# First head of a graph attention layer: two half tiles to a buffer, and a new order of the work around them

## Chip, core, metric

One core of a Trainium2 chip. The metric is the device time of one execution in microseconds (us), as the median of several runs. The profile is of one further execution, whose own time is given beside its span.

## What is computed

Four graph layers, one after the other, on a matrix `x` of 2708 nodes by 512 features with a 0/1 adjacency matrix of 2708 x 2708. Each layer adds to `x` what it computes from `h = relu(layernorm(x))`. The change is in layer 2, graph attention with 8 heads of 64 features:

```python
Wh = jnp.einsum('nd,hdo->hno', x, W)
f1 = jnp.einsum('hno,ho->hn', Wh, a1)
f2 = jnp.einsum('hno,ho->hn', Wh, a2)
e = jax.nn.leaky_relu(f1[:, :, None] + f2[:, None, :], negative_slope=ALPHA)
e = jnp.where(adj[None, :, :] > 0, e, NEG_INF)
attention = jax.nn.softmax(e, axis=-1)
h_prime = jnp.einsum('hnm,hmo->hno', attention, Wh)
out = jax.nn.elu(h_prime)
```

Here `x` stands for that layer's `h`. Layers 0, 1 and 3 multiply the adjacency matrix (layer 1 a part of it) with a matrix of 512 columns.

## The kernel before

**Attention without exponentials of matrices.** The exponential of a leaky ReLU of a sum is a maximum of two products of one factor for the node of the row and one for the node of the column. So the exponentials are taken of vectors only: `exps_nodes` makes `er` from f1, `exps2` makes `ef` and `ec` from f2. The row factors of a head are turned by TensorE and sent to a DRAM row `rT` (`row2`: a transpose into `f_ps`, a copy by ScalarE into a tile `row`, and a DMA that ScalarE issues), and one DMA (`load_row1`, tile `rb`, issued by SyncE) spreads a head's row over all 128 partitions. A weight tile for 128 neighbours is then one VectorE instruction (`make`): the maximum of the row and `ec`, times the 0/1 pattern `vT` of the adjacency matrix, into a tile `t2` of 128 x 2708 with four buffers (`TILES`).

**Units and steps.** A unit is a head with a range of columns. The first and the last head are split in two halves of columns at `cut` (1408 and 1300 columns), the six heads between them are whole, so there are ten units. Each has 22 steps, one for each chunk of 128 nodes (NC = 22; the last has 20 nodes). In step s the planner's loop first issues the load of the features for step s + 6 (in groups of three), the scaling of the features for step s + 3 (`scale`, ScalarE, tile `whs`, four buffers), the weights for step s + 3 (`make`), then TensorE's products of step s (`multiply`: 16 instructions for the features into `av`, 8 for the row sums into `sums`, 32 columns wide so that four run beside each other in the array), and then what `plan` holds for the step. In the middle heads, and in the first half of the last one, 17 of 22 steps take their row sums from a comparison that ScalarE makes (`compare`, tile `b`).

**Neighbour sums.** Beside the first head's 44 steps, TensorE also counts over neighbours (`count_neighbors`, `adj_sums`, 17 sets of 8 products). Each set needs four pieces of the pattern in bf16 (`mask`, ScalarE, tile `x` with five buffers; the fourth piece of later sets is made by VectorE). `fourths` are the borders of the pieces.

**Early and late chunks.** The first EARLY = 11 chunks get their exponentials and rows while layer 2's dense part still runs (`rows2`, six steps behind the loads of that part). In the dense part a chunk c is loaded at step c, normalized, turned, multiplied (`product2`, at c + 3, which also makes the products with a1 and a2: `wh_a`, one on VectorE and one on GpSimd) and summed (`sums2` at c + 4, VectorE, into `f` and `f12`). At chunk `LATE` = 17 the first features are loaded, and at chunks 18, 19 and 20 the first three scalings and weights are made. The exponentials and rows of the late chunks are planned for the first head's steps 4 to 9, `split` (bf16 parts of the factors, on ScalarE and VectorE) for step 9, and the load of the second half's row for step 10.

**Tails.** The 20 nodes of the last chunk are put together for the six middle heads into one tile of 120 rows: `load_tails` (30 small DMAs and more on SyncE's queue, planned for step 12), `exp_tails` on ScalarE (step 30) and `make_tails` on VectorE (step 36).

**What sets the order.** The program's order is a priority. A scheduler at compile time puts each engine's instructions into a fixed order by a model of when each is ready, so an instruction can be ahead of its place in the code: in the trace the tails' scaling runs at 855.0 us, some ten steps before its place. `tc.issue_after(ins)` puts what follows behind `ins` on that engine's queue. Each engine then works through its own fixed order and waits at an instruction whose inputs or buffer are not ready.

The change touches `rows2` with `LATE`, `make`, `load_row1`, `row2`, `mask`, `cut`, the list `stages2`, and the plan and the loop over `steps`.

Of the kernel before, what the change touches and what calls it, by code (L numbers as in the profile page):

```python
# [8 lines left out]
F32 = mybir.dt.float32  # L9
F32R = mybir.dt.float32r  # L10
BF16 = mybir.dt.bfloat16
# [9 lines left out]
P = 128  # L21

R = 128
# [3 lines left out]
TILES = 4  # L27
# [17 lines left out]
def fast_layers(  # L45
# [36 lines left out]
    nc = tc.nc  # L82
    N, D = x_in.shape
    H, _, O = w2.shape
    NC = -(-N // R)
# [6 lines left out]
    def rows(c):  # L92
        return min(R, N - c * R)
# [18 lines left out]
    EARLY = NC // 2  # L112
# [363 lines left out]
    with ExitStack() as ring_ctx:  # L476
# [20 lines left out]
        def save2(c):  # L497
            move(nc.scalar, x2[c * R : c * R + rows(c), :], sums1.pop(c)[: rows(c)])
# [9 lines left out]
        with tc.tile_pool(name="l0", bufs=2) as wk, ExitStack() as ctx_l0:  # L508
            units = [(g, m) for g in range(len(groups)) for m in range(NC)]
# [213 lines left out]
            for i in range(2):  # L723
                first_unit = (1 + 2 * i) * NC
                at(first_unit - 10, fusion.load, i)
                steps = [(fusion.turn, i, f) for f in range(NF) if i]
# [174 lines left out]
        def before1(c):  # L901
# [8 lines left out]
            x2,  # L910
            lambda *args: product2(*args),
            False,
            [(3, lambda c: save_last2(c)), (4, lambda c: sums2(c)), (6, lambda c: rows2(c))],
            scalar=True,
        )
        ahead = [(m, emit_step, step, NC, stages2) for step, m in enumerate(AHEAD)]
# [14 lines left out]
    ABOVE = 1.0 + 2.0**-21  # L931
    S = 32

    cut = EARLY * R // 8 * 8
    units = [(h, 0, N) for h in range(H)]
    units[-1:] = [(H - 1, 0, cut), (H - 1, cut, N)]
    units[:1] = [(0, 0, cut), (0, cut, N)]
# [3 lines left out]
    def in_tails(u, m):  # L941
        return m == NC - 1 and units[u][0] in middle

    steps = [
        (u, m)
        for u in range(len(units))
        for m in ((NC - 1, *range(NC - 1)) if 1 < u < len(units) - 1 else range(NC))
    ]

    def by_side(u, m):  # L950
        return 1 < u < len(units) - 1 and m in BY_SIDE
# [11 lines left out]
    at = at_ctx.enter_context(tc.tile_pool(name="att", bufs=1, reuse_waits="tile"))  # L963
# [10 lines left out]
    nc.gpsimd.memset(one6, 0.0)  # L974
    nc.gpsimd.memset(one6[:, 6:7], 1.0)
    row, weight, wh, whs, acc, sides, made, scaled = {}, {}, {}, {}, {}, {}, [], {}

    def load_row1(h, lo, hi):

        if lo == 0:  # L980
            row[h] = at.tile([R, N], F32, name="rb", bufs=2)
        src = rT[h : h + 1, lo:hi]
        nc.sync.dma_start(
            row[h][:, lo:hi],
            bass.AP(tensor=src.tensor, offset=src.offset, ap=[[0, R], [1, hi - lo]]),
        )

    LINES = len(middle) * last_rows
    assert LINES <= P
# [55 lines left out]
    def scale(s):  # L1045

        u, m = steps[s]
        h, q = units[u][0], rows(m)
        if in_tails(u, m):
            whs[s] = tails_w[:LINES, middle.index(h)]  # L1050
            return
        t = at.tile([R, O + S], F32, name="whs", bufs=4)
        by = ef[:q, m, h : h + 1]
        ins = nc.scalar.activation(t[:q, :O], wh.pop((u, m))[:q], AF.Copy, scale=by)  # L1054
        if not by_side(u, m):
            ins = nc.scalar.activation(t[:q, O:], one6[:q], AF.Copy, scale=by)
        scaled[s] = ins.ins
        whs[s] = t[:q]

    def make(s):  # L1060
        u, m = steps[s]
        h, lo, hi = units[u]
        q = rows(m)
        g, k = where[m]
        if in_tails(u, m):
            weight[s] = tails_row[:LINES]
            made.append(made[-1])
            return
        t = at.tile([R, N], F32, name="t2", bufs=TILES)
        ins = nc.vector.scalar_tensor_tensor(  # L1070
            t[:q, : hi - lo],
            row[h][:q, lo:hi],
            ec[:q, m, h : h + 1],
            vT[g][:q, k, lo:hi],
            op0=ALU.max,
            op1=ALU.mult,
        )
        weight[s] = t[:q]
        made.append(ins.ins)
# [47 lines left out]
    def sums2(c):  # L1127
        n = rows(c)
        f = small.tile([P, 2, H], F32, name="f")

        with tc.issue_after(firsts[min(c + 1, NC - 1)]):
            for i in range(2):
                t = products.pop((c, i))
                nc.vector.tensor_reduce(f[:n, i, :], t[:n, :, : O // (1 + i)], AX.X, ALU.add)  # L1134

        nc.vector.tensor_scalar(
            f12[:n, c, :],
            f[:n].rearrange("p i h -> p (i h)"),
            F_MAX + 1.0,
            -F_MAX - 1.0,  # L1140
            op0=ALU.min,
            op1=ALU.max,
        )

    def row2(c):
        pf = ps.tile([P, R], F32, name="f_ps", tag="ps")
        nc.tensor.transpose(pf[:H], er[:, c], ident[:R, :R])
        r = at.tile([H, R], F32, name="row", bufs=2)
        nc.scalar.copy(r, pf[:H])
        nc.scalar.dma_start(rT[:, c * R : (c + 1) * R], r)  # L1150

    def exps_nodes(cs):
        nc.scalar.activation(er[:, cs], f12[:R, cs, :H], AF.Exp, scale=1.0 - SLOPE2)

    def exps2(cs):
        nc.scalar.activation(ef[:, cs], f12[:R, cs, H:], AF.Exp)
        nc.scalar.activation(ec[:, cs], f12[:R, cs, H:], AF.Exp, scale=SLOPE2 - 1.0)
# [27 lines left out]
                    parts2[:, at_i[0] : at_i[-1] + 1 : len(kinds), i, heads], src  # L1185
                )

    LATE = NC - 5
    early_rows = [(0, EARLY // 2 + 1), (EARLY // 2 + 1, EARLY)]

    def rows2(c):
        for first, end in early_rows:
            if c == end - 1:
                exps_nodes(slice(first, end))
            for n in range(2):
                if first <= first + 2 * (c - end + 1) + n < end and c >= end - 1:
                    row2(first + 2 * (c - end + 1) + n)
        if c == EARLY - 1:
            exps2(slice(0, EARLY))
        if c == EARLY + 1:  # L1200
            load_row1(*units[0])
            split(0, EARLY)

        if c == LATE:
            load_wh(0)
            load_wh(GROUP)
        if LATE < c <= LATE + 3:
            scale(len(made))
            make(len(made))

    def save_last2(c):
        if c < len(spans[-1]):
            save2(spans[-1][c])
# [5 lines left out]
    tails = tails_ctx.enter_context(  # L1219
        tc.tile_pool(name="tails", bufs=1, side="right", reuse_waits="tile")  # L1220
    )
# [140 lines left out]
    fourths = [0, cut // 2, cut, (cut + N) // 2, N]  # L1362
    counted, masks = [], {}
# [4 lines left out]
    def mask(i, j):  # L1368
        m = BY_SIDE[i]
        q = rows(m)  # L1370
        g, k = where[m]
        own = slice(fourths[j], fourths[j + 1])
        n = own.stop - own.start
        if j == 3 and m >= EARLY:
            t = masks[i, j] = tails.tile([P, fourths[1]], BF16, name="mask", bufs=2)
            nc.vector.tensor_copy(t[:q, :n], vT[g][:q, k, own])
            return
        t = masks[i, j] = common.tile([P, D], F32, name="x", bufs=XBUFS).bitcast(BF16)
        nc.scalar.copy(t[:q, :n], vT[g][:q, k, own])
# [40 lines left out]
    def behind(s, fn, *args):  # L1420
        plan.setdefault(s, []).append((fn, args))

    behind(4, exps_nodes, slice(EARLY, NC))
    behind(4, exps2, slice(EARLY, NC))
    for c in range(EARLY, NC):
        behind(4 + (c - EARLY) // 2, row2, c)
    behind(10, load_row1, *units[1])
    behind(9, split, EARLY, NC)
    behind(12, load_tails)
    behind(30, exp_tails)  # L1430
    behind(36, make_tails)
    behind(30, load_l3_weights)
# [41 lines left out]
    for s in range(len(steps)):  # L1474
        if s == (len(units) - 3) * NC + 1:
            tails_ctx.close()
            first3 = ctx.enter_context(
                tc.tile_pool(name="first3", bufs=1, side="right", reuse_waits="tile")
            )
            rings3 = [first3]  # L1480
            b3 = first3.tile([P, D], F32, name="b3")
            nc.sync.dma_start(
                b3, bass.AP(tensor=bias3.tensor, offset=bias3.offset, ap=[[0, P], [1, D]])
            )
            e3_ctx = ctx.enter_context(ExitStack())
            e3 = e3_ctx.enter_context(
                tc.tile_pool(name="e3", bufs=2, side="right", reuse_waits="tile")
            )
        if s + 6 < len(steps) and (s + 6) % NC % GROUP == 0:
            load_wh(s + 6)  # L1490
        if s + 3 < len(steps):
            scale(s + 3)
            make(s + 3)
        if s + 1 < len(steps):
            compare(s + 1)
        multiply(s)
        multiply_sides(s - 1)
        for fn, args in plan.pop(s, ()):
            if fn in (load_l3_weights, spread_nodes, split):
                with tc.issue_after(made[s]):  # L1500
                    fn(*args)
            elif fn is mask:
                with tc.issue_after(scaled[s + 2]), tc.issue_after(made[s]):
                    fn(*args)
            else:
                fn(*args)
# [715 lines left out]
```

## Time and profile before

| what | us |
|---|---|
| median of 3 runs (1745.71 to 1747.05) | 1746.12 |
| the profiled execution | 1746.28 |
| its span from first to last instruction | 1744.5 |
| TensorE busy in the span | 1721.5 (99%) |
| VectorE busy | 1317.9 (76%) |
| ScalarE busy | 845.4 (48%) |
| GpSimd busy | 248.3 (14%) |

On the time axis of the span, layer 2's dense part ends at 810.6 us, the first half of the first head runs to 863, the second to 903, and the heads to 1356. The engines are called PE (TensorE's products), PEld (its weight loads), DVE (VectorE), ACT (ScalarE), POOL (GpSimd) and SP (SyncE, of which only the DMA queue matters here). A stretch in which PE is busy is not one in which it works at its peak, since its ends are modelled, and its clock can be lowered: the share of the full clock that it was granted is a column of its own. Waits are attributed to what came last.

Durations that come up again, in the trace before:

| instruction | us |
|---|---|
| weights of 128 x 1408 (DVE) | 1.60 from start to next start |
| weights of 128 x 1300 | 1.49 |
| weights of 128 x 2708 | 3.03 |
| piece of the pattern (ACT, `x`) | 0.76 |
| scaling of a step's features (ACT, two instructions) | 0.34 and 0.31 |
| row: copy (ACT) and issue of its DMA | 0.25 and 0.27 |
| loading ACT's table for the exponential | 1.28 |
| broadcast of the first half's row, from issue to first use | 4.3 |

### The profile page before, as it was taken

Reading aid. Unit: us, or ns where it says so; the run is one execution under the profiler, and the core shown is the slowest. Engines: PE = TensorE matmul, PEld = TensorE weight load, DVE = VectorE, ACT = ScalarE, POOL = GpSimd, SP = SyncE. Lnnn points to the kernel's source line nnn. Section 1 sums busy time; section 2 is a strip of 40 time slices with the busy share of each in tenths; the row PEclk is TensorE's granted clock in tenths of the full one; section 3 lists DMA queues with packets and bytes.
Section 4 is the critical chain, followed back from the end, with each engine's and each line's share of the span. In section 5 each row is a group of like instructions: output and inputs, shape, how many; then the busy total and the mean of one; then the engine's idle time right before and its main releaser. Section 6 shows DMA issues by size and latency. Waiting matters only on the chain.

```text
span 1744.5 us, 29430 instructions
## 1 busy us (share of the span) xinstructions
PE 1721.5 (99%) x11280; PEld 1074.9 (62%) x11280; DVE 1317.9 (76%) x1902; ACT 845.4 (48%) x1556; POOL 248.3 (14%) x252
## 2 busy tenths in 40 slices
PE   8999999999999999999999999999999999999998
PEld 5567777744458888644675665433434544588886
DVE  7759889865555556888899999999999787633334
ACT  5446767622210000266878888888794656400000
POOL 1003323311111111365000000000001222100000
PEclk9999999999999999999999999999999999999999
DMA  8446666444551111342420221022022444313221
GB/s 292 136 122 198 205 204 188 139 115 124 121 142 49 49 49 53 118 129 94 131 64 15 61 64 47 26 65 66 16 68 77 135 132 128 113 36 109 74 73 41
DMA packets 167227, 177.37 MB, mean 102 GB/s; under 512 B 84127, under 2 KB 106591, under 8 KB 166060
## 3 DMA queue, kind: packets, MB, share of 16 engines
q1 hardware_dynamic: 144428, 131.99, 27.4%
q10 hardware_dynamic: 18808, 33.37, 5.0%
q0 software_dynamic: 3840, 10.03, 1.5%
q8 instruction: 90, 1.47, 0.4%
q14 instruction: 61, 0.50, 0.1%
HBM read 111.64 MB, written 55.36 MB: 96 GB/s over the span
## 4 chain that ended last, share of the span: by engine, by line
PE 42%; DVE 9%; issue 3%; ACT 2%; DMA 2%; SPq 1%; POOL 0%; ACTq 0%; DVEq 0%; POOLq 0%
PE av L1315 15%; PE acc L425 12%; DVE t L1070 7%; PE self_ps L187 4%; PE nb_ps L187 4%; PE sums L1315 3%; DMA x<-x 1%; PE hT_ps L246 1%; PE wh_ps L187 1%; DVE wh_a L1117 1%; ACT b L1088 1%; PE av_ps L1253 1%; DVE f L1134 1%; DVE ln_st L219 0%; DMA rb<-rT 0%
## 5 line engine op out<-in xcount | busy, mean ns | idle before, releaser
L1070 DVE SCALAR_TENSOR_TENSOR t<-rb,ec,vT 128x2708 f32<-128x2708 f32 (+2 forms) x214 | 510.8, 2456 | 8.3 <-PE sums L1315 6.4
L1315 PE MATMUL av<-t,whs 128*32 128x451 f32 (+5 forms) x4432 | 444.6, 514 | 6.0 <-DVE t L1070 4.7
L425 PE MATMUL acc<-halves,kt 128*128 128x512 f32 x1848 | 423.6, 390 | 1.0 <-DVE kt L873 1.0
L425 PEld LDWEIGHTS acc<-halves,kt 128*128 128x128 f32 x1848 | 346.1, 188 | 75.3 <-DVE kt L873 2.6
L1088 ACT ACTIVATE b<-t,eb 128x2708 bf16<-128x2708 f32 (+1 forms) x119 | 285.1, 2396 | 33.2 <-DVE t L1070 33.1
L1315 PEld LDWEIGHTS av<-t,whs 128*32 128x32 f32 (+1 forms) x4432 | 192.4, 110 | 169.6 <-issue 119.4
L425 PE MATMUL acc<-halves,ar 128*128 128x512 f32 x924 | 243.8, 414 | 0.0
L425 PEld LDWEIGHTS acc<-halves,ar 128*128 128x128 f32 x924 | 172.5, 188 | 58.3 <-issue 20.8
L223 ACT ACTIVATE ln_rs<-ln_mv,eps 128x1 f32<-128x1 f32 x88 | 25.7, 295 | 305.9 <-DMA x<-x 199.0
L873 DVE SCALAR_TENSOR_TENSOR kt<-lastr,index,vT 128x512 fp32r<-128x512 int16 (+3 forms) x154 | 112.8, 747 | 72.4 <-PE acc L425 72.2
L1539 DVE CAST kt<-vT 128x512 fp32r<-128x512 uint8 (+3 forms) x154 | 56.4, 368 | 130.6 <-PE acc L425 130.6
L1267 POOL TENSOR_SCALAR z<-y 128x512 f32<-128x512 f32 x22 | 43.7, 1987 | 628.7 <-DVE y L1260 623.1
L558 DVE TENSOR_TENSOR_SCAN cum<-ai,deg 128x512 int16<-128x512 int32 (+2 forms) x110 | 128.3, 1170 | 0.0
L601 ACT ACTIVATE cum<-cum,limit 128x512 int16<-128x512 int16 (+3 forms) x132 | 88.0, 667 | 51.5 <-DVE deg L566 49.4
L1315 PE MATMUL sums<-t,whs 128*32 128x325 f32 (+4 forms) x952 | 103.9, 449 | 0.0
L1054 ACT ACTIVATE whs<-wh,ef 128x64 f32<-128x64 f32 x214 | 72.5, 341 | 53.0 <-PE sums L1315 18.9
L219 DVE BATCH_NORM_STATS2 ln_st<-x 128x6 f32<-128x512 f32 x88 | 60.5, 689 | 49.7 <-DMA x<-x 35.1
L187 PE MATMUL wh_ps<-w2s,hT 128*128 128x512 f32 x168 | 76.0, 595 | 0.9 <-ACT hT L248 0.9
L187 PE MATMUL h_ps<-w0s,hT 128*128 128x512 f32 x168 | 76.5, 598 | 0.0
L1315 PE MATMUL sums<-b,parts 128*32 128x338 bf16 (+2 forms) x884 | 76.2, 308 | 0.0
L552 ACT ACTIVATE ar<-ai 128x512 fp32r<-128x512 int32 (+2 forms) x132 | 75.0, 568 | 1.8 <-DMA ai<-in_adj 1.3
L187 PE MATMUL self_ps<-wfs,hT 128*128 128x512 f32 x168 | 75.7, 593 | 0.0
(211 smaller groups left out, 1956.2 us busy)
## 6 DMA issues: line engine op xcount, KB each, us to landing
x<-x SPq DMA_DIRECT2D x105, 256.0 KB
ai<-in_adj SPq DMA_DIRECT2D x84, 256.0 KB
x<-x ACTq DMA_DIRECT2D x84, 256.0 KB
x<-in_x SPq DMA_DIRECT2D x42, 256.0 KB
rb<-rT SPq DMA_DIRECT2D x7, 1354.0 KB
wh<-whd SPq DMA_DIRECT2D x63, 96.0 KB
packed<-two POOLq DMA_DIRECT2D x44, 128.0 KB, 3.0
whd<-wh SPq DMA_DIRECT2D x21, 256.0 KB
```

The costliest lines, as they stand in the source:

```text
L187: nc.tensor.matmul(po[:n], lhsT[:, f, :n], w[:, f, :], start=(f == 0), stop=(f == NF - 1))
L219: nc.vector.bn_stats(st[:n], xc[:n])
L425: nc.tensor.matmul(acc[:R], weight[:, k * R : (k + 1) * R], parts[:, i, :], start=(m == 0 and i == 0), stop=(m == NC - 1),)
L552: nc.scalar.activation(ar[:, :gw], ai[:, :gw], AF.Square, accum_out=squares[:R, m, g : g + 1])
L558: nc.vector.tensor_tensor_scan(cum[:n, :gw], ai[:n, :gw], ai[:n, :gw], 0.0 if g == 0 else deg[:n, m : m + 1], op0=ALU.add, op1=ALU.max,)
L601: nc.scalar.activation(cum[:n, :gw], cum[:n, :gw], AF.Sign, bias=limit[:n], scale=-1.0, accum_out=signs[:n, m, g : g + 1],)
L873: nc.vector.scalar_tensor_tensor(by_chunk(kt, cs), lastr[:, cs[0] * R : (cs[-1] + 1) * R].rearrange("p (c r) -> p c r", r=R), index[:R, m ...
L1054: ins = nc.scalar.activation(t[:q, :O], wh.pop((u, m))[:q], AF.Copy, scale=by)
L1070: ins = nc.vector.scalar_tensor_tensor(t[:q, : hi - lo], row[h][:q, lo:hi], ec[:q, m, h : h + 1], vT[g][:q, k, lo:hi], op0=ALU.max, op1=AL ...
L1088: nc.scalar.activation(b[:q, : hi - lo], weight[s][:, : hi - lo], AF.Sigmoid, bias=eb[:q, m, h : h + 1], scale=STEEP,)
L1315: nc.tensor.matmul(p[j * S : (j + 1) * S, : b - a], lhsT, rhs[:, part * size + a : part * size + b], start=(s % NC == 0), stop=(s % NC == ...
L1539: nc.vector.tensor_copy(by_chunk(kt, cs), pattern(m, cs))
```

## The change

The first head is cut at 1352 columns and no longer at 1408, so that two half tiles (1352 and 1356 columns) fit into one weight tile: odd steps of unit 0 use the second half of the buffer of the step before. In the dense part, scaling and weights start at chunk 13 and not at 18, with up to three scalings and eight weights (`LATE + 2 * TILES`). Within a step of the dense part `rows2` comes ahead of the sums, and the last chunk's sums are put behind the seventh weight. In the loop, weights may run up to five steps ahead until the early ones are made. The late chunks' exponentials are planned three steps later and put behind the scaling of step s + 2 = 9; their rows are planned three steps later and have three buffers; the second row's load moves from step 10 to 13, `split` from 9 to 12, and `load_tails` from 12 to 19 and behind the second row's load. `cut` is also that of the last head.

```diff
-            [(3, lambda c: save_last2(c)), (4, lambda c: sums2(c)), (6, lambda c: rows2(c))],
+            [(3, lambda c: save_last2(c)), (6, lambda c: rows2(c)), (4, lambda c: last_sums2(c))],
...
-    cut = EARLY * R // 8 * 8
+    cut = N // 2 // 8 * 8
+    assert cut <= EARLY * R and 2 * cut <= N
...
+    row_loads = []
...
-        nc.sync.dma_start(
+        ins = nc.sync.dma_start(
...
+        row_loads.append(ins.ins)
...
-        t = at.tile([R, N], F32, name="t2", bufs=TILES)
+        if u == 0 and m % 2:
+            t = weight[s - 1, cut]
+        else:
+            t = at.tile([R, N], F32, name="t2", bufs=TILES)
+            if u == 0:
+                weight[s, cut] = t[:, cut:]
...
+    def last_sums2(c):
+        with ExitStack() as behind:
+            if c == NC - 1:
+                behind.enter_context(tc.issue_after(made[6]))
+            sums2(c)
...
-        r = at.tile([H, R], F32, name="row", bufs=2)
+        r = at.tile([H, R], F32, name="row", bufs=3)
...
-    LATE = NC - 5
+    LATE = EARLY + 1
...
         if LATE < c <= LATE + 3:
-            scale(len(made))
+            scale(len(whs))
+        if LATE < c <= LATE + 2 * TILES:
             make(len(made))
...
-            t = masks[i, j] = tails.tile([P, fourths[1]], BF16, name="mask", bufs=2)
+            t = masks[i, j] = tails.tile([P, N - fourths[3]], BF16, name="mask", bufs=2)
...
-    behind(4, exps_nodes, slice(EARLY, NC))
-    behind(4, exps2, slice(EARLY, NC))
+    behind(7, exps_nodes, slice(EARLY, NC))
+    behind(7, exps2, slice(EARLY, NC))
     for c in range(EARLY, NC):
-        behind(4 + (c - EARLY) // 2, row2, c)
-    behind(10, load_row1, *units[1])
-    behind(9, split, EARLY, NC)
-    behind(12, load_tails)
+        behind(7 + (c - EARLY) // 2, row2, c)
+    behind(13, load_row1, *units[1])
+    behind(12, split, EARLY, NC)
+    behind(19, load_tails)
...
             scale(s + 3)
-            make(s + 3)
+        while len(made) <= min(s + (5 if len(made) < EARLY else 3), len(steps) - 1):
+            make(len(made))
...
+            elif fn in (exps_nodes, exps2):
+                with tc.issue_after(scaled[s + 2]):
+                    fn(*args)
+            elif fn is load_tails:
+                with tc.issue_after(row_loads[1]):
+                    fn(*args)
```

## The prediction

> **What bounds the kernel now.** I read the stretch from layer 2's dense part to the middle heads as a table of stretches first, since the page's shares of the span (PE 99%) hide short stalls; then the timelines of PE, VectorE (DVE), ScalarE (ACT) and the sync queue (SP) around each gap. Columns of the table: stretch, its length, busy time (instructions) of PE, PEld, DVE, ACT, POOL, then the granted clock, DMA share, GB/s.
>
> ```profile
> 811.00:830.00 19.00, 16.35 (x196) 7.30 (x192) 17.93 (x25) 12.12 (x33) 8.02 (x7) 0.91 0.30 86
> 830.00:847.00 17.00, 15.36 (x201) 7.40 (x197) 12.16 (x11) 14.11 (x45) 0.00 (x0) 1.00 0.44 124
> 847.00:863.00 16.00, 15.97 (x223) 11.49 (x215) 13.81 (x10) 14.11 (x33) 0.00 (x0) 1.00 0.44 100
> 863.00:883.00 20.00, 19.44 (x295) 17.16 (x299) 20.00 (x16) 17.15 (x44) 0.00 (x0) 1.00 0.41 116
> 883.00:903.00 20.00, 20.00 (x312) 16.29 (x306) 19.47 (x14) 14.82 (x30) 0.00 (x0) 1.00 0.29 89
> 903.00:923.00 20.00, 19.68 (x227) 8.17 (x223) 19.20 (x8) 16.33 (x25) 0.00 (x0) 1.00 0.17 43
> 963.00:1063.00 100.00, 100.00 (x1230) 68.62 (x1224) 100.00 (x35) 84.12 (x78) 0.00 (x0) 1.00 0.18 51
> ```
>
> Two things show here. First, from about 920 on DVE is 100% busy beside PE: its stream of weights sets the pace of the middle heads, so time gained earlier counts only if DVE's stream comes earlier too. Second, the idle time lies in the first head. PE lacks 2.65 + 1.64 + 0.03 + 0.56 + 0.32 = 5.2 us in 811 to 923, DVE 1.07 + 4.84 + 2.19 + 0.53 + 0.80 = 9.4 us. The timelines name the gaps (start, length, engine, line, what; last the idle time and its releaser): PE's two kinds, then DVE's and ACT's part in the first one.
>
> ```profile
> 821.24 2.39 PE L1315 MATMUL av<-t,whs 128*32 128x352 f32 x16 [2.65 <-DVE t L1070]
> 839.78 0.44 PE L1391 MATMUL adj_sums<-x,parts 128*24 128x325 bf16 x5 [1.01 <-ACT x L1379]
> ```
> ```profile
> 809.60 1.67 DVE L1070 SCALAR_TENSOR_TENSOR t<-rb,ec,vT 128x1408 f32<-128x1408 f32 x1
> ...
> 819.52 1.66 DVE L1070 SCALAR_TENSOR_TENSOR t<-rb,ec,vT 128x1408 f32<-128x1408 f32 x1
> ```
> ```profile
> 821.30 0.28 ACT L1153 ACTIVATE er<-f 128x88 f32<-128x88 f32 x1 [3.95 <-DVE f L1136]
> ```
> ```profile
> 822.00:823.00 1.00, 1.00 (x12) 0.42 (x8) 1.00 (x2) 1.00 (x7) 0.00 (x0) 0.50 0.01 0
> 825.00:826.00 1.00, 1.00 (x14) 0.42 (x16) 1.00 (x2) 0.98 (x4) 0.00 (x0) 1.00 0.11 22
> ```
>
> Four weights are all that four buffers hold. After the fourth (809.60) DVE does the last chunks' products and sums until 819.5, PE eats the four by 818.6 and stands 2.65 us; then its clock is 0.50 from about 821.5 to 824.9, which costs 3.4 x 0.5 = 1.7 us more. ACT, at the head of whose queue an exponential waits for the last sums, loses 3.95 us, and its masks come late at 839 (1.01) and 845 (0.63).
>
> [...]
>
> **The change, part by part.** The sum is made against the profiled execution, 1746.28 us (span 1744.5 and 1.78 around it), 0.16 above the median of 1746.12.
>
> Two halves to a buffer. Eight half tiles fit where four did. The row's broadcast still lands at 799.0 at the earliest I can justify: it is issued at 794.72, 1.99 us after the DMA of the last early row, which ACT issues at 792.73; moving the start from chunk 17 to 12 doesn't touch this. From 799.01 to 821.19 DVE does five weights (5 x 1.60) and has 0.78 idle, so the last sums cost 22.18 - 8.0 - 0.78 = 13.4 us. A half of 1352 costs 1.54 us (1.60 at 1408, 1.49 at 1300). Nine weights and all sums are done at 799.0 + 13.4 + 9 x 1.54 = 826.3. PE starts its first step at 810.6, a step takes 1.77 us at 352 columns (810.60 to 812.40, less records that overlap) and so 1.70 at 338; with three sets of neighbour sums (0.3 each) and the first transposes (0.43 a pair, from 2.20 us steps against 1.77) it wants the ninth at 810.6 + 8 x 1.70 + 0.9 + 0.4 = 825.5. So the stall of 2.65 becomes about 0.8 at step 8, at most 1.5, too short to lower the clock (1.01 at 839 didn't: 1.00 in 830 to 847). Gain 2.65 + 1.7 - 0.8 = 3.5 us. Only three or four of the eight are made before 811; the point is that DVE can go on.
>
> Last sums behind the seventh weight, rows ahead of sums in a chunk. No instruction is added. Queued behind the waiting sums on DVE are only later weights; on other engines the exponentials of the late chunks, due at step 7 now. Sums end near 824.5, exponentials need 1.28 for the table and some 0.6, so weight 11 can be made from 826.5, when DVE has just finished weight 8: hidden. The cover is thin: if the sums end 3 us later, PE waits about 1.
>
> Exponentials behind step 9's scaling. ACT's 3.95 us are filled with masks and scalings instead. The wait is for scaling 9, that is for step 5's multiply, about 821.7; ACT still waits up to 2.5 us for the sums. Gain: part of the 1.64 of mask stalls.
>
> Rows from three buffers. 11 copies (0.25) and 11 DMA issues (0.27) stay, moved from steps 4 to 9 to steps 7 to 12. A third buffer removes ACT's waits for a row's DMA (idle before the row copies and scalings 0.3 to 0.7 each, some 2 us between 834 and 839).
>
> ACT together: in 811 to 863 it works 12.12 + 14.11 + 14.11 = 40.3 us, and about 3 us more for the DMA issues, which aren't counted as busy; PE's time for the unit without stalls is 22 x 1.70 + 2.6 + 2.5 = 42.5. That is full, so I keep half of the ACT stalls (1.64 + 0.42 at the change of unit, halved: 1.0) and take 1.0 as gained; bounds 2.1 gained, 2 lost.
>
> Columns from one half to the other. 56 columns less in each first half and more in each second: PE 22 x 0.07 = 1.5 us earlier and later, sum zero. In the last head the second half takes its sums on PE in fp32 (0.55 us for 8) and the first mostly in bf16 (0.30): (0.55 - 0.30) x 56/1350 x 17 steps = 0.2 us lost. Taken: 0.2.
>
> Second row load at step 13 and the tails behind it. SP: the tails' 30 issues take 819.62 to 838.5 now, and the second row load is issued behind them at 844.08. With the last late row sent near 836 it can go at 838 and land by 843; weight 22 is due on DVE near 848. Hidden by 5 us; free. The tails move to 838 to 857, their scaling is due at step 30 (about 868) and runs at 854.7 now. Free if ACT has them in time.
>
> DVE's split operations. Idle before them 0.93 and less, waiting for ACT; now they meet a fuller ACT: -1 to +1, taken 0.
>
> DVE as a check: from 799 on it can gain no more than its 9.4 us of idleness. PE can gain at most 5.2 + 1.7 = 6.9. From 6.9 I take the new 0.8, the kept 1.0 and the 0.2: about 5, and as DVE has 9.4 to give, it follows. I add 0.1 for earlier masks: 5.2 us, 1746.28 - 5.2 = 1741.1.
>
> **Rivals.** (a) Likeliest, 0.60: 1741.1; its own range 1739.3 to 1743.0.
> (b) ACT becomes the bound of the unit, 0.18. Rows, masks and splits meet in steps 7 to 13, while PE no longer pauses. For: 43 of 42.5 us. Against: the 3.95 us are given back. It takes 2 to 4 us at the neighbour sums: 1744.0.
> (c) More than I count, 0.10: no new stall, all ACT waits gone, the row a little earlier: 6.9 and 0.7 (DVE idle before 799.01): 1738.7.
> (d) Slower, 0.12: the tails' scaling on ACT stands where it did (854.7, some 6 us earlier by PE's progress: 848.7) while SP is still issuing their loads until 857, landing 859.5. ACT is held 11 us, everything behind it too; scalings and masks reach 2 steps (4 us) ahead, so PE stands 7, runs 1.7 at half clock, and ACT then catches up at little more than PE's rate, 1.5 more: 1741.1 + 10.2 = 1751.3. It decides from a hold of about 8 us. Against: SP took these issues between other work before without holding ACT over 0.6.
> That the eight aren't made early is inside (a): the order on DVE then gives a first stall of 1 to 2 us.
>
> **How the numbers follow.** About 0.2% (3.5 us) is what a measurement of this kernel tells from no change: faster is under 1742.6, slower over 1749.6. (a) gives 0.54 faster and 0.06 same; (b) 0.02, 0.15, 0.01; (c) 0.10 faster; (d) 0.01 same, 0.11 slower. Sums: 0.66, 0.22, 0.12. The range takes in (a), (b), most of (c) and the near end of (d): 1737.5 to 1748.
>
> **What would show it.** Right: no idle PE over 1.5 us in 811 to 860, clock 1.00 there, two weights to a buffer with at least seven done by 818, exponentials after the ninth scaling, the second row load ahead of the tails, DVE's idleness to 923 down from 9.4 to about 4. Wrong: ACT waiting for sums or tails over 3 us, neighbour sums waiting over 2 us in total, the row's broadcast later than 799, or a gain that is gone before DVE's full stretch ends at 1322.

## The result and the profile after

The changed kernel takes 1754.86 us (median of 6 runs, 1754.42 to 1756.88) against 1746.36 for the kernel before beside it (1745.45 to 1747.86): ratio 1.0052, 95% interval 1.0042 to 1.0063. It is slower by about 8.5 us; 1741.1 was forecast. The profiled execution took 1754.42 us, its span 1752.5.

First the same table of stretches, of the kernel after (stretch, length, busy time and instructions of PE, PEld, DVE, ACT, POOL, then clock, DMA share, GB/s):

```profile
811.00:830.00 19.00, 16.95 (x238) 8.98 (x234) 19.00 (x22) 14.09 (x35) 10.01 (x6) 1.00 0.39 125
830.00:847.00 17.00, 14.80 (x200) 7.33 (x204) 17.00 (x13) 11.38 (x33) 0.00 (x0) 1.00 0.17 52
847.00:863.00 16.00, 16.00 (x181) 8.93 (x177) 7.36 (x9) 15.58 (x43) 0.00 (x0) 0.89 0.23 54
863.00:883.00 20.00, 13.83 (x184) 6.08 (x180) 14.58 (x11) 9.85 (x27) 0.00 (x0) 0.87 0.42 101
883.00:903.00 20.00, 20.00 (x289) 11.30 (x285) 18.11 (x15) 14.04 (x37) 0.00 (x0) 0.96 0.23 71
```

811 to 830 went as planned: DVE has no gap (17.93 of 19.00 before) and the clock stays at 1.00 (0.91 before). The loss is in three later rows: clock 0.89 in 847 to 863, PE only 13.83 of 20 in 863 to 883, and 0.87 and 0.96 after that. The timelines name the gaps (start, length, engine, line, what; last the idle time and its releaser). PE has four of note:

```profile
822.14 1.34 PE L1330 MATMUL av<-t,whs 128*32 128x338 f32 x16 [0.90 <-DVE t L1078]
825.21 1.35 PE L1330 MATMUL av<-t,whs 128*32 128x338 f32 x16 [1.15 <-DVE t L1078]
846.66 0.32 PE L1406 MATMUL adj_sums<-x,parts 128*24 128x338 bf16 x2 [2.19 <-ACT x L1394]
879.94 1.69 PE L1330 MATMUL av<-tails_row,tails_w 120*32 120x451 f32 x2 [6.17 <-DMA avT<-out]
```

The first two are new waits for weights at steps 6 and 7, where a single one of 0.8 at step 8 was forecast. The third is a mask that comes late. The fourth is the largest: the compiled order has two products of the tails in the middle of the second half, and their weights are not there. The releaser printed is an eviction's DMA that ended last by the profile; DVE and ACT show the real chain.

```profile
876.70 3.04 DVE L1021 SCALAR_TENSOR_TENSOR tails_row<-tails_row,tails_f,tails_v 120x2708 f32<-120x2708 f32 x1 [1.67 <-ACT tails_f L1017]
```
```profile
845.48 0.58 ACT L1187 CAST parts<-rest 128x88 bf16<-128x88 f32 x1 [2.71 <-DVE rest L1189]
...
876.37 0.20 ACT L1016 ACTIVATE tails_f<-tails_f 120x1 f32<-120x1 f32 x1 [7.20 <-DMA tails_w<-whd]
```

PE waits for DVE's weights of the tails (876.70 + 3.04 = 879.74), DVE for ACT's exponential at 876.37, and ACT has stood 7.20 us for the tails' loads. SyncE's queue says why they are late:

```profile
842.34 0.34 SPq L985 DMA_DIRECT2D rb<-rT  x1
846.88 0.36 SPq L1043 DMA_DIRECT2D wh<-whd  x1
847.30 0.41 SPq L1003 DMA_DIRECT2D tails_row<-rT  x1
847.81 0.77 SPq L1007 DMA_DIRECT2D tails_v<-vT  x1
855.16 0.38 SPq L1043 DMA_DIRECT2D wh<-whd  x1
855.64 0.75 SPq L1008 DMA_DIRECT2D tails_f<-f  x1
...
874.70 0.73 SPq L1012 DMA_DIRECT2D tails_w<-one  x1
875.54 2.42 SPq L1372 DMA_DIRECT2D avT<-out  x4
```

A load of features holds the queue behind the second row until 846.88, the tails begin at 847.3, the queue then stands 6.6 us at the next load of features (848.6 to 855.16), and the remaining 28 issues run nearly without a pause until 875.4. The trace puts the waits of both loads down to ACT's scalings, which free the buffer that they fill. Before, 24 of the 30 issues ran from 819.62 to 838.7 and the six of the rows from 844.47 to 846.8, and ACT came to the exponential at 854.72 without a wait.

How far TensorE has come, by the first product of each stretch, is the measure used below. The last column is the last group of row sums of the heads.

| kernel | first step | second half | third unit (tails) | end of the heads |
|---|---|---|---|---|
| before | 810.60 | 863.38 | 902.77 | 1355.66 |
| after | 809.82 | 861.84 | 911.8 | 1363.81 |

Step 8 begins at 832.35 before and at 827.65 after, 4.7 us earlier. At the second half 1.5 us are left of it, which are no more than the 56 columns moved (22 x 0.07). At the third unit TensorE is 9.0 behind.

### The profile page after: what moved, and what is told of

It is laid out like the page before. It is cut to its first block, busy times and chain, and to the rows that moved or that the text cites. A ratio compares the mean times of both kernels' runs of the same rounds, so it can differ in the third digit from the quotient of the medians.

```text
span 1752.5 us, 29433 instructions
## 1 busy us (share of the span) xinstructions
PE 1724.3 (98%) x11280; PEld 1059.0 (60%) x11280; DVE 1320.6 (75%) x1902; ACT 843.6 (48%) x1556; POOL 252.0 (14%) x252
## 4 chain that ended last, share of the span: by engine, by line
PE 85%; DVE 9%; ACT 2%; issue 1%; SPq 1%; DMA 1%; ACTq 0%; DVEq 0%
PE acc L425 37%; PE av L1330 17%; PE nb_ps L187 8%; DVE t L1078 6%; PE h_ps L187 4%; PE line_ps L187 4%; PE sums L1330 4%; PE self_ps L187 4%; PE hT_ps L246 2%; PE fused_ps L371 2%; PE wh_ps L187 1%; DVE wh_a L1125 1%; DVE f L1142 1%; ACT b L1096 1%; PE av_ps L1268 1%
## 5 line engine op out<-in xcount | busy, mean ns | idle before, releaser
L1330 PEld LDWEIGHTS av<-t,whs 128*32 128x32 f32 (+1 forms) x4432 | 183.5, 110 | 174.7 <-issue 130.6
L1330 PE MATMUL sums<-t,whs 128*32 128x339 f32 (+2 forms) x952 | 103.7, 449 | 0.0
L187 PE MATMUL nb_ps<-wfn,hT 128*128 128x512 f32 x168 | 75.6, 593 | 0.0
```

The source lines that it names most:

```text
L187: nc.tensor.matmul(po[:n], lhsT[:, f, :n], w[:, f, :], start=(f == 0), stop=(f == NF - 1))
L1330: nc.tensor.matmul(p[j * S : (j + 1) * S, : b - a], lhsT, rhs[:, part * size + a : part * size + b], start=(s % NC == 0), stop=(s % NC == ...
```

## The experiments

Two theories after the result. **Queue:** the tails' loads on SyncE hold ACT, then DVE, then PE; take them off that queue and some 7 us come back. **ScalarE:** masks, rows, scaling and split fill the first head, so what the halves win is lost again inside the unit. The rival to both: the halves' own new waits (2.05 us) and the order of weights and sums. In the expectations below, theory A is the queue, theory B one part of what fills ScalarE (the split that makes a mask late), and theory C the rival.

| run | built on | edit | us | ratio to before, 95% |
|---|---|---|---|---|
| e1 | after | tails at step 12, not behind the row | 1758.2 | 1.0056 to 1.0083 |
| e2 | after | split at step 9 | 1755.25 | 1.0038 to 1.0066 |
| e3 | after | both | 1758.64 | 1.0058 to 1.0085 |
| e4 | before | tails at step 19 behind the row | 1749.46 | 1.0011 to 1.0025 |
| e5 | after | tails' small loads on GpSimd | 1747.58 | 1.0002 to 1.0019 |
| e6 | before | the same | 1744.96 | 0.9983 to 1.0000 |
| e7 | e5 | split at step 9 | 1747.32 | 1.0000 to 1.0017 |
| e8 | e7 | four masks more on VectorE | 1745.17 | 0.9986 to 1.0003 |
| e9 | e7 | eight masks more on VectorE | 1744.85 | 0.9984 to 1.0000 |
| e10 | e6 | four masks more on VectorE | 1743.18 | 0.9974 to 0.9989 |
| e11 | e9 | split at step 17 | 1742.52 | 0.9975 to 0.9988 |
| e12 | e11 | no halves | 1742.47 | 0.9974 to 0.9989 |

The kernel before took 1745.7 to 1746.1 beside them.

### Tails and split back at their places (e1, e2, e3)

```diff
-    behind(19, load_tails)
+    behind(12, load_tails)
...
-            elif fn is load_tails:
-                with tc.issue_after(row_loads[1]):
-                    fn(*args)
```

That is e1; e2 has `behind(9, split, EARLY, NC)`, e3 both.

> The changed kernel with the tails' loads back at step 12 and not behind the second row load. Theory A (SyncE's queue: the tails' 30 issues stand behind the second row load and in front of feature loads and evictions, ScalarE is held at the tails' exponential, PE stands 6.2 us and runs 4.6 us at half clock, 8.5 us in all): PE's stall of 6.17 us near 880 is gone, time near 1754.9 - 8.5 = 1746.4. Theory B (the split's VectorE steps behind 13 weights make a mask late, 2.2 us and 3.5 us at half clock, 3.9 in all) and theory C (weights made ahead are themselves the loss, as they push back the sums): the 6.17 us move elsewhere, time above 1752. The second row load can now come late, since it is issued behind the tails: up to 4 us.

> The changed kernel with the split planned at step 9 as before and not at 12. Theory B: fewer weights stand in front of its first VectorE step, the 2.19 us stall at the neighbour sums near 846 and the half clock after it go, time near 1754.9 - 3.9 = 1751.0. Theories A and C: 1754.9 within 1 us, since the stall near 880 sets the end (a gain in front of it is eaten by the wait for the tails' loads).

> The changed kernel with the tails' loads back at step 12 and the split back at step 9; everything else of the change stays. A and B together: 1754.9 - 8.5 - 3.9 = 1742.5, faster than before by about 4 us, which is the gain that I had forecast from the eight halves less a new first stall of 2 us. Theory C: not below 1746.4.

e1 missed theory A's number by about 12 us, and e3 that of A and B together by about 16. e2 came out as theories A and C had it. Taken alone, the three do not speak for A: C had also allowed for e1 and e3, and it takes e4 and e5 to decide. In e1 the early place is no cure: the timeline of SyncE, PE and DVE of e1 shows the tails at the head of the queue, waiting for the last sums, which the change has made later.

```profile
824.01 0.83 SPq L1007 DMA_DIRECT2D tails_v<-vT  x1
...
853.66 0.36 SPq L985 DMA_DIRECT2D rb<-rT  x1
```
```profile
835.68 0.27 PE L1161 MATMUL f_ps<-ident,er 128*8 128x128 f32 x1 [3.28 <-ACT row L1163]
...
871.02 2.49 PE L1330 MATMUL av<-t,whs 128*32 128x339 f32 x16 [4.50 <-ACT x L1394]
```
```profile
866.30 3.04 DVE L1021 SCALAR_TENSOR_TENSOR tails_row<-tails_row,tails_f,tails_v 120x2708 f32<-120x2708 f32 x1 [10.87 <-ACT tails_f L1017]
```

They start at 824.01 instead of 819.62, and their issues now delay the features (ACT stands 5.8 us, PE 3.28) and the second row, issued at 853.66 instead of 842.34. At the tails PE still stands 4.50 us, but for another reason: ACT reaches the exponential at 865.97 and waits for no load there; it comes late itself. DVE's weights of the tails wait for it, and the first weight of the second half, which PE needs at 871.02, stands behind them. Two stalls in place of one: 3.3 us more. e3 has the same two, 3.21 and 6.36. e2 takes the mask's 2.19 us down to 0.15, at the price of 1.69 at a row's transpose, and the end doesn't move, because the wait for the tails (5.17) lies behind it. While that wait ends last, no other edit can be read.

### The tails' place in the kernel before (e4)

The edit is the change's own two lines for `load_tails`, with `row_loads`, in the kernel before.

> The kernel before with one edit: the tails' loads planned at step 19 and put behind the second row load. Theory A: slower by 6 to 9 us, 1752 to 1755, with ScalarE waiting for the tails' loads over 5 us in the second half of the first head. Theories B and C: 1746.4 within 1.5 us.

3.4 us are lost there too, less than the 6 to 9 expected: ACT stands 3.72 us for the tails' loads and PE 4.37 at 875.30. So the late place costs by itself, without the halves. It costs less than in the kernel after, since SyncE's relief in the first half pays part of it back: the mask stalls there, 1.64 us in the kernel before, shrink to 0.36.

### The small loads on GpSimd's queue (e5, e6)

```diff
-            nc.sync.dma_start(tails_v[own], vT[g][:last_rows, k, :N])
+            nc.gpsimd.dma_start(tails_v[own], vT[g][:last_rows, k, :N])
...
+    def load_tail_rows():
...
-    behind(19, load_tails)
+    behind(8, load_tails)
+    behind(19, load_tail_rows)
```

All 24 small loads go to GpSimd's queue at step 8; the six row loads stay on SyncE behind the second row's load. In e6 the steps are 5 and 12.

> The changed kernel with the 24 small tails' DMAs (pattern, factors, features, ones) on GpSimd's queue, which is idle after 820 us, planned at step 8; the six row loads of the tails stay on SyncE at step 19 behind the second row load. Every other queue order is that of the changed kernel. Theory A': it is SyncE's queue, wherever the tails stand in it (in E1 the first of them waited for the last sums and held the feature loads; in the changed kernel they come late): now ScalarE does not wait for tails, PE's 6.17 us and the half clock after it go: 1754.9 - 8.5 = 1746.4, with the mask stall near 846 left. Theory C (weights made ahead are the loss): not below 1752.

> The kernel before with the same edit (24 small DMAs on GpSimd's queue from step 5, row loads of the tails on SyncE at step 12). Theory A': SyncE is not what PE waited for in the first head before (weights and masks were), so 1746.1 within 2 us; a row copy's wait of 0.4 to 0.6 us and a part of the 1.64 us of mask stalls can go: 1744.5 to 1746.5. If GpSimd's queue itself is slow, ScalarE waits for the tails at their exponential near 855: up to 1755.

e5 wins 7.3 of the 8.5 us and ends 1.2 above theory A's 1746.4. In its timeline ACT's exponential of the tails has no wait any more, and of PE's four waits three are left:

```profile
869.49 0.20 ACT L1020 ACTIVATE tails_f<-tails_f 120x1 f32<-120x1 f32 x1
```
```profile
822.57 1.35 PE L1334 MATMUL av<-t,whs 128*32 128x338 f32 x16 [1.26 <-DVE t L1082]
825.64 1.35 PE L1334 MATMUL av<-t,whs 128*32 128x338 f32 x16 [1.15 <-DVE t L1082]
847.09 0.39 PE L1410 MATMUL adj_sums<-x,parts 128*24 128x338 bf16 x2 [2.19 <-ACT x L1398]
```

The third unit begins at 902.84, as in the kernel before (902.77). So the queue theory holds. The edit moves the loads to another queue and to an earlier step at once; e1 shows that an earlier step alone, on SyncE's queue, is no cure, and a late step on GpSimd's queue was not run. The same edit makes the kernel before 1.0 us faster (e6), which is at the edge of what its interval tells. With the tails out of the way in both, the changed order is still 2.6 us behind the old one: the rest of the diff has not won anything either.

### ScalarE and the split (e7 to e11)

> E5 with the split at step 9. Theory B, which E2 could not show as the wait for the tails' loads came behind it: the mask stall of 2.19 us and 1.75 us of half clock go, 1746.4 - 3.9 = 1742.5. If a stall of PE at the rows' transposes takes its place (1.7 us in E2): 1744 to 1746.

e7 missed: 0.3 us, no more than the runs' scatter. The mask's stall is gone (0.16), and a stall at a row's transpose has come in its place, as in e2:

```profile
839.03 0.27 PE L1165 MATMUL f_ps<-ident,er 128*8 128x128 f32 x1 [1.69 <-ACT row L1167]
```

Behind it ACT is busy 15.90 of 16 us in 847 to 863, and PE's steps 14 to 18 take 2.2 to 3 us each, where e9 below shows 1.71. No gap of PE in these steps is long enough to be listed: it waits a little at many products. The next runs therefore take work off ACT.

```diff
-        if j == 3 and m >= EARLY:
+        if j == 3 and m >= 5:
```

This is e8 and, on e6, e10; e9 has `if j == 3 and m >= 5 or j == 2 and 5 <= m < EARLY`.

> The kernel of e7 (tails' small loads on GpSimd, second split at step 9), and the fourth mask piece of the blocks 5, 6, 8 and 9 made by VectorE as it is for the later blocks: four casts of 0.70 us leave ScalarE in steps 11 to 20, VectorE gains four of 0.51. If ScalarE bounds the middle of the first head, 1.5 to 2.8 us are won on e7's 1747.3: 1744.5 to 1745.8, and the steps 14 to 18, which take 2.2 to 3 us each there, get shorter. If TensorE's own work or VectorE's weights bound it, 1747.3 within 0.5.

> As e8, with the third piece of these blocks on VectorE as well: eight casts, 5.6 us off ScalarE and 4.1 onto VectorE, whose idle 8 us of waiting for the second row load can hold them. ScalarE as the bound: 1742.5 to 1744.5, below e8 by 1 to 2. Not the bound: 1747.3 or more, since masks on VectorE then stand behind weights.

> The control: the kernel of e6 (the order of before, tails' small loads on GpSimd) with the same four casts moved. There the masks are less late (stalls of 1.64 us in the kernel before), so ScalarE as the bound gives less: 0.3 to 1.6 us below e6's 1745.0, 1743.4 to 1744.7. Not the bound: 1745.0 within 0.4.

2.15 us from four casts of 0.70, 0.3 more from eight (which was expected to give 1 to 2, and is not told from nothing), and 1.8 in the order of before (0.3 to 1.6 expected). ScalarE did bound the middle of the first head, in both orders. In e9 the steps after 840 are 1.71 us apart (start of three successive steps in PE's timeline), TensorE's own pace at 338 columns:

```profile
842.82 1.31 PE L1334 MATMUL av<-t,whs 128*32 128x338 f32 x16
...
844.52 1.32 PE L1334 MATMUL av<-t,whs 128*32 128x338 f32 x16
...
846.23 1.32 PE L1334 MATMUL av<-t,whs 128*32 128x338 f32 x16
```

What is left in e9 is one wait of ACT and the stall of PE behind it:

```profile
837.44 0.58 ACT L1191 CAST parts<-rest 128x88 bf16<-128x88 f32 x1 [2.30 <-DVE rest L1193]
```
```profile
838.64 0.30 PE L1410 MATMUL adj_sums<-x,parts 128*24 128x339 bf16 x1 [1.86 <-ACT x L1398]
```

The first difference of `split` stands on DVE behind seven weights in a row; in the kernel after it stands behind thirteen (DVE's timeline there):

```profile
825.16 20.06 DVE L1078 SCALAR_TENSOR_TENSOR t<-rb,ec,vT 128x1352 f32<-128x1352 f32 x13
845.15 0.29 DVE L1189 TENSOR_TENSOR rest<-ef,parts 128x88 f32<-128x88 f32 x1
```

e11 moves the split to step 17, where DVE has made its weights:

> The kernel of e9 with the second split at step 17 in place of 9, where VectorE has made its weights and waits for the second row load. In e9 ScalarE waits 2.30 us there for VectorE's first difference, behind seven weights in a row, and TensorE then 1.86 for a mask. If that wait is what is left of the loss in the first head, both go and 1.2 to 2.0 us are won on e9's 1744.9: 1742.9 to 1743.7. If ScalarE or TensorE is full anyway, the stall moves on and the time stays at 1744.9 within 0.5.

2.3 us between the two medians, or 2.05 when each is taken against the kernel before beside it: the upper end of what was expected. PE's remaining waits are the two for weights, 0.99 and 1.15, and 0.74 at a mask.

### The halves alone (e12)

```diff
-        if u == 0 and m % 2:
-            t = weight[s - 1, cut]
-        else:
-            t = at.tile([R, N], F32, name="t2", bufs=TILES)
-            if u == 0:
-                weight[s, cut] = t[:, cut:]
+        t = at.tile([R, N], F32, name="t2", bufs=TILES)
...
-                behind.enter_context(tc.issue_after(made[6]))
+                behind.enter_context(tc.issue_after(made[3]))
...
-        if LATE < c <= LATE + 2 * TILES:
+        if LATE < c <= LATE + TILES:
...
-        while len(made) <= min(s + (5 if len(made) < EARLY else 3), len(steps) - 1):
+        while len(made) <= min(s + 3, len(steps) - 1):
```

> The kernel of e11 with one weight to a buffer again: four weights in layer 2's dense part in place of eight, each three steps ahead, the last sums behind the fourth. What the halves are worth by themselves, once SyncE and ScalarE are out of the way: if it is what the forecast took (2.65 us of stall and 1.7 of half clock against 0.8), 3.5 us are lost, about 1746.5 to 1747.5 and a stall of 2 to 3 us behind the fourth weight. If the halves only move the loss, within 1 us of e11.

No difference: 1742.47 and 1742.52. The run takes out the shared buffer with all that belongs to it (eight early weights, the lead of five, the place of the last sums); the other parts of the change stay. PE's waits of e11 and then of e12:

```profile
823.06 1.35 PE L1334 MATMUL av<-t,whs 128*32 128x338 f32 x16 [0.99 <-DVE t L1082]
826.12 1.35 PE L1334 MATMUL av<-t,whs 128*32 128x338 f32 x16 [1.15 <-DVE t L1082]
```
```profile
819.26 1.34 PE L1329 MATMUL av<-t,whs 128*32 128x338 f32 x16 [1.33 <-DVE t L1077]
827.63 0.38 PE L1160 MATMUL f_ps<-ident,er 128*8 128x128 f32 x2 [0.76 <-ACT er L1166]
```

0.99 + 1.15 = 2.14 us with the halves (and the 0.74 at a mask later), 1.33 + 0.76 = 2.09 without. DVE has the same weights and sums to make in either order and hardly a gap meanwhile (busy 19.00 of 19 us in 811 to 830 in e11, 18.09 in e12). With halves the weights come first and PE waits at steps 6 and 7 for weights behind the sums; without them the last reduction ends at 817.7 instead of 824.5, and PE waits once for the fifth weight and once for the exponentials. A buffer more lets DVE work in another order, not less.

With four buffers PE stands 1.33 us at the fifth weight here and 2.65 in the kernel before. The difference is mostly the row's. DVE's first and fifth weight of e12, and the first of the kernel before:

```profile
797.37 1.62 DVE L1077 SCALAR_TENSOR_TENSOR t<-rb,ec,vT 128x1352 f32<-128x1352 f32 x1 [0.82 <-DMA rb<-rT]
...
817.60 1.60 DVE L1077 SCALAR_TENSOR_TENSOR t<-rb,ec,vT 128x1352 f32<-128x1352 f32 x1
```
```profile
799.01 1.69 DVE L1070 SCALAR_TENSOR_TENSOR t<-rb,ec,vT 128x1408 f32<-128x1408 f32 x1 [0.70 <-DMA rb<-rT]
```

From the first to the fifth weight DVE takes 20.2 us in e12 and 20.5 before (799.01 to 819.52). But it begins 12.8 us ahead of PE's first step in e12 and 11.6 ahead before. These 1.2 us are an effect of the new order that e12 keeps; which part of it brings them was not tested.

The time axis shows one thing more:

| kernel | first step | second half | third unit | end of the heads |
|---|---|---|---|---|
| e9 | 810.77 | 859.74 | 900.33 | 1353.81 |
| e10 | 810.32 | 860.78 | 899.71 | 1352.63 |
| e11 | 810.65 | 857.88 | 898.49 | 1351.92 |
| e12 | 810.21 | 855.81 | 897.39 | 1351.32 |

e12 is 2.1 us ahead of e11 at the second half, 1.1 at the third unit, 0.6 at the end of the heads. TensorE's lead isn't worth its face value, since VectorE's stream sets the pace later: DVE is busy 140.00 of 140 us in 923 to 1063, in before, after, e11 and e12 alike. Both streams stand in one table of 797 to 923 (columns as above), for before, after, e11 and e12:

```profile
797.00:923.00 126.00, 120.80 (x1484) 74.30 (x1486) 115.84 (x94) 93.95 (x214) 19.26 (x13) 0.99 0.33 93
```
```profile
797.00:923.00 126.00, 115.30 (x1380) 58.11 (x1382) 109.49 (x87) 86.33 (x205) 20.20 (x11) 0.96 0.30 87
```
```profile
797.00:923.00 126.00, 122.19 (x1531) 60.22 (x1533) 124.07 (x101) 89.91 (x206) 33.98 (x36) 1.00 0.32 90
```
```profile
797.00:923.00 126.00, 122.16 (x1536) 63.78 (x1538) 122.13 (x101) 90.24 (x206) 28.85 (x36) 1.00 0.31 89
```

DVE's idleness is 10.2 us before, 16.5 after, 1.9 in e11, 3.9 in e12. With the halves DVE's stream is 1.9 us further by 923, without them TensorE is further, and at the end the two are even. That these cancel is read from the tables, not tested by a run of its own.

e10 shows it too, for a larger lead. It has the old order, and in it a first stall of 2.53 us with half clock behind it; its masks and its split differ from e12's as well. Counted from the first step, and less the 1.5 us of its 56 columns more, it is 3.3 us behind e12 at the second half, 2.2 at the third unit, 1.2 at the end of the heads, and 0.7 in the median. About a third of e12's lead is left at the end of the heads.

e10, e11 and e12 all beat the kernel before by 0.11 to 0.26%. Their intervals overlap, so whether the rest of the change (rows ahead of the sums, later exponentials, three row buffers) adds anything to e10, which has none of it, stays open.

## Why the prediction was wrong

**The step that failed: "The tails move to 838 to 857 ... Free if ACT has them in time."** They moved to 847 to 875, and ACT did not have them in time. The consumer came when it was forecast: ACT stood at the exponential from 869.2, where "about 868" had been said. It was the loads that ended 18.4 us late. They began 9.3 late: the last late row left ACT at 841.08 and not near 836, the second row went out at 842.34 and not at 838, and a feature load held the queue after it. The next feature load took 6.6 us more. And the issues themselves took some 2.5 longer, as the 19 us read from 819.62 to 838.5 had been those of 24 issues and not of 30. The feature loads' waits at the head of the queue are in no term of the prediction. The cost is measured: 7.3 us (e5 against after), and 3.4 in the order of before (e4).

It was rival (d)'s mechanism, given 0.12 and 1751.3. Its sizes were of the right order: ACT held 11 us by forecast and 7.2 measured, PE standing 7 and 6.2, half clock 1.7 and 2.3 (the clock is 0.50 in 881 to 884 and recovers by 884.6). Its place was later, and its argument against, "SP took these issues between other work before without holding ACT over 0.6", was void: before, ACT came to the exponential 8 us after the last of these issues (854.72 against 846.8), so that the queue could not hold it.

**The second failing step: "take 1.0 as gained" for ScalarE, with "That is full" in the same paragraph.** Without the tails' wait (e5) the second half begins 52.36 us after the first step, against 52.78 before. 3.5 + 1.0 from the prediction's sum and 1.5 from the moved columns should have made 6.0; 0.4 came. So 5.6 us are lost again inside the unit. They are rival (b)'s, "neighbour sums", forecast at 2 to 4. The runs name what fills the unit: moving masks off ScalarE wins 2.5 us (e7 to e9), of which four masks win 1.8 in the old order too (e6 to e10), and moving the split from behind DVE's weights wins 2.3 (e9 to e11). They are not a partition of the 5.6, as the halves' part of the forecast was itself too large (below). "DVE's split operations ... taken 0" had looked only at ACT as the one to be waited for; it was DVE that came late, once eight and more weights ran ahead of it.

**"Gain 2.65 + 1.7 - 0.8 = 3.5 us" for the halves.** The mechanism ran as described and nearly on time: ninth weight and all sums done at 826.7 (forecast 826.3), no half clock, TensorE 4.7 us ahead at step 8 (0.8 of it from an earlier first step, 0.6 from the columns). The row landed at 796.9, 2.1 earlier than allowed for, and the new stall was 2.05 and not 0.8, as two weights and not one lie behind the late sums. What failed is the inference that the four buffers caused the 2.65: e12 has four buffers and stands 1.33, mostly because the row comes earlier, a gain that the prediction had put at nothing ("doesn't touch this"). With the way clear the halves are worth nothing beside it (e11, e12). In the order of before they were not run alone.

**Smaller terms.** The sum has a slip: 6.9 less 0.8, 1.0 and 0.2, with 0.1 added, is 5.0 and not 5.2, and the parts themselves (3.5 + 1.0 - 0.2) make 4.3. Either still forecasts a gain of over 4 us. ACT's 3.95 us in front of the exponentials went, as forecast. The third row buffer did not remove ACT's pauses: idle times of 0.56, 0.55, 0.55, 1.11 and 0.53 us remain at the rows between 827 and 840, beside issues of 0.62 to 1.20 us for two DMAs; they are the issues' own time. The second row's load was free: DVE took its first weight of the second half at 850.18 without a wait. The check on DVE was sound as a check: its idleness was to fall, by 5 us; it rose by 6 (797 to 923), and the time rose with it.

## What to carry to other kernels

Before a block of DMAs is called free at a new place, go through its queue in order, with every load that may stand at its head (here two feature loads held SyncE's queue, the second for 6.6 us), and compare its end with the place of its first consumer in that engine's compiled order; then name who stands behind that consumer. A stall that a producer releases after a run of its own work can be a sum of work and not of buffers: add up what the producer does between two fixed points, and a further buffer pays only if that sum gets smaller or the order ends earlier for the one who waits (here PE waited 2.14 us with the halves and 2.09 without). And where an engine is as full as the unit is long, count no gain inside that unit until work is taken off it (here 0.4 us came of 6.0; four casts of 0.70 us taken off ScalarE won 2.15).

## What the runs showed of the hardware that was not expected

In these traces the idle time alone does not tell when the clock drops. In the kernel after, 2.19 us of idleness at 844.5 to 846.7 are followed by half clock:

```profile
848.00:849.00 1.00, 1.00 (x9) 0.52 (x9) 0.21 (x2) 1.00 (x3) 0.00 (x0) 0.50 0.91 266
```

In e6 a wait of 2.51 us leaves the clock at 1.00 (820 to 824), and it falls some forty microseconds later (1.00 in 858 to 860, 0.50 in 862 to 864), after 0.42 us of idleness:

```profile
821.29 1.39 PE L1319 MATMUL av<-t,whs 128*32 128x352 f32 x16 [2.51 <-DVE t L1074]
...
861.58 2.32 PE L1319 MATMUL av<-t,whs 128*32 128x325 f32 x16 [0.42 <-ACT whs L1058]
```
```profile
820.00:824.00 4.00, 2.71 (x34) 1.06 (x38) 4.00 (x4) 2.65 (x11) 3.23 (x7) 1.00 0.78 259
...
862.00:864.00 2.00, 2.00 (x20) 0.87 (x16) 2.00 (x2) 2.00 (x6) 0.00 (x0) 0.50 0.54 135
```

In e10, 2.53 us at nearly the same place do lower it:

```profile
820.84 2.24 PE L1319 MATMUL av<-t,whs 128*32 128x352 f32 x16 [2.53 <-DVE t L1074]
```
```profile
822.00:824.00 2.00, 2.00 (x16) 0.42 (x8) 2.00 (x3) 2.00 (x7) 2.00 (x5) 0.50 0.45 138
```

And in e2 it falls at about 861.8 (0.50 in 862 to 864) with no idle time of PE listed near. There and in e6 the products of the last chunk, with its 20 rows, run just ahead; whether that matters was not tested. In the kernel before they run ahead of the same 0.42 us of idleness, and the clock stays at 1.00 (863 to 883):

```profile
863.38 1.30 PE L1315 MATMUL av<-t,whs 128*32 128x325 f32 x16 [0.42 <-ACT whs L1054]
```

So equal waits ended differently: 0.42 us before and in e6, and 2.51 us in e6 against 2.53 in e10. What decides it was not shown. Where the clock fell behind a stall of 2.19 to 2.65 us (before, after, e10), it stayed at half for about 3.4 us: 821.5 to 824.9 before, 847.1 to 850.5 after, and the same in e10 by the mean clocks of 820 to 826 (0.81, 0.50 and 0.84). Such a stall therefore cost TensorE either itself (e6) or some 3.4 x 0.5 = 1.7 us more at its place. Each trace is of one execution, so whether a kernel does the same in every execution isn't known, and by the end of the heads less of it may be left, as e10 shows.
